# Two moves in a two-layer kernel: the position strips load behind the third time tile's twelfth slot tile, and the delta pairs are copied after the score masks

## The chip, the cores and the metric

The program runs on one core of one Trainium2 chip. The metric is device time of one execution in microseconds (us), the median of several runs. Before the change it is 2380.52 us (three runs, 2380.49 to 2381.03).

The core has five engines with their own instruction queues: TensorE (PE in the profile; its weight loads are PEld), VectorE (DVE), ScalarE (ACT), GpSimd (POOL) and SyncE (SP). Each works through its queue in the order in which the program was written out; an instruction that waits holds up everything behind it on its engine. DMA transfers are issued from SP's and from POOL's queue. The profile counts them as two DMA queues, q1 (hardware, SP) and q0 (software, POOL), served by 16 DMA engines.

## The reference

The input is `x`, 8 batches of 512 positions by 256 features, float32. Two transformer-like layers follow each other:

- Layer 0, attention: a delta-rule recurrence over the 512 positions with a 16 by 16 state for each of 16 heads and 8 batches (`delta = v - M k`, `M += beta k delta`, output `q M`), then RMS norm and a projection.
- Layer 0, feed-forward: a top-1 router over 8 experts, each 256 to 1024 to 256 with relu.
- Layer 1, attention: causal softmax attention with a relative position bias looked up by distance.
- Layer 1, feed-forward: 8 experts of 256 by 256, weighted by a thresholded softmax.

Before each part there is a layer norm with shift and scale from a small modulation matrix, and behind each a gated residual sum.

## The kernel before

**Time tiles.** The 512 positions are cut into four time tiles of 128 (`i` = 0 to 3; "the third time tile" is i = 2). `scan(i)` runs the recurrence of one tile, 128 steps of four VectorE operations each, for all batches and heads at once. While VectorE scans tile i, the other engines do the rest for tile i-1, cut into pieces with a due time in scan steps. `run` sorts the pieces by due time and issues a piece behind the scan step that it is due at. The scan of tile 3 is the last one; what is left of tile 2, all of tile 3's attention and routing, and then tile 3's experts come behind it, in the order of their due times alone.

**What follows a tile's scan** (`follow`): `attend(i)` turns keys and queries (`turn`, L593 writes `qT`), makes scores (`scores`, L607), masks them and copies the delta pairs (`mask`), weighs them (`weigh`, L663), projects, and adds to the residual rows `x1` (`rest`, L722 and L723); POOL then stores each batch's rows `x1[b]` to HBM (L724). The rows were loaded from the input by `tokens` (L563, on SP). For tiles 0 to 2, ScalarE copies the scores out of PSUM and POOL masks them (L642) and copies the pairs (L630). For tile 3, VectorE does both (L644 and L630). There is one `pair` tile, which `weigh` of the batch before still reads.

`route(i)` normalises `x1` in place (L781 on ScalarE, which must wait until the store L724 of that batch has read the rows), makes the router's logits, ranks the rows by expert and scatters them by an indirect DMA (L895) into 15 *slot tiles* of 128 rows, each of one expert.

`experts(i)` goes over the 15 slot tiles `j`: load the rows (L928, on SP, two buffers), turn them (L931), first expert matrix (L943), relu (L952), second matrix (L961), bias (L967, POOL), store (L968, POOL). The expert's two weight matrices, 1.05 and 1.18 MB, are fetched for each slot tile by indirect DMAs from POOL (L916), two buffers each. In the scan of tile 3 the slot tiles 0 to 11 of tile 2 are due from step 73 on, 4.3 steps apart; slot tiles 12, 13 and 14 (`rest`) are due at 58, 68 and 71 behind the scan.

**Gathers.** A tile's expert outputs are gathered back row by row (L976), multiplied by the gate (L1005) and added into the residual rows in HBM by an accumulating DMA (L1006), all issued by POOL, with two buffers `yrow`. For tiles 0 and 1 this is 16 gathers, and all of them stand behind the last scan, right behind slot tile 11 of tile 2 in POOL's order.

**Layer 1's constants.** `load1` (due at step 54 of the last scan) loads layer 1's weights. The position bias comes as `strips`, one row of 16 heads by 512 distances for each partition, 4.19 MB in all. `load_strips(p0)` loads it for 8 partitions at a time (L1070 on SP: 256 KB as 128 pieces of 2 KB), 16 loads. They are due at steps 56, 60, ... 116 of the last scan. The strips are read first by layer 1's scores (L1148). `place1` later loads layer 1's expert weights `ew` (L278, two loads of 1 MB on SP). The first rows for layer 1, `xs_first`, are loaded on SP (L972), and their statistics are made by VectorE (L186).

Of the kernel before, what the change touches and what calls it, by code (L numbers as in the profile page):

```python
# [19 lines left out]
P = 128  # L20
B = 8
S = 512
D = 256
NH = 16
# [6 lines left out]
STRIP = 640  # L31
# [26 lines left out]
COPIES = 8  # L58
# [5 lines left out]
def tile_two_layers(ctx: ExitStack, tc: tile.TileContext, t: dict, out: bass.AP):  # L64
    nc = tc.nc
# [9 lines left out]
    def bank():  # L75
        n_ps[0] += 1
        return banks[0].tile([P, 512], F32, tag="ps", name=f"ps{n_ps[0]}")
# [5 lines left out]
    strip_d = dram.tile([NH, COPIES, STRIP], F32, tag="strip_d", name="strip_d")  # L83
    hs_d = [dram.tile([NSLOT * P, D], F32, tag=f"hs{i}", name=f"hs{i}") for i in range(NT)]
# [17 lines left out]
    with tc.tile_pool(name="setup", bufs=2) as sp:  # L102
        for layer in range(2):
# [9 lines left out]
            for branch in range(2):  # L113
                for part in range(2):
# [11 lines left out]
                    got = pm[:, : 2 * B].rearrange("p (h b) -> p h b", h=2)  # L126
# [92 lines left out]
    w1 = {}  # L219
# [131 lines left out]
    with ExitStack() as l0:  # L351
# [11 lines left out]
        def free(i):  # L363

            return nc.vector if i == NT - 1 else nc.gpsimd
# [34 lines left out]
        pair = w0.tile([P, NH // 2, 3, HD], F32, name="pair")  # L400
# [152 lines left out]
        def attend(i, qk, V, x1, norms):  # L553
# [3 lines left out]
            got = {}  # L557
            ve = free(i)
# [68 lines left out]

            def mask(b):
                psts = got["s", b]
                ve.tensor_copy(  # L630
                    pair[:, :, 0:3:2, :],
                    got["dtok"][:, b * NH : (b + 1) * NH, :].rearrange(
                        "p (j o) d -> p j o d", o=2
                    ),
                )
                sts = []
                for r in range(4):
                    st = ap.tile([P, 4, P], F32, tag="stk", name=f"stk{i}_{b}_{r}", bufs=4)
                    before = strict.unsqueeze(1).to_broadcast([P, 4, P])
                    if i < NT - 1:  # L640
                        nc.scalar.copy(st, psts[r].rearrange("p (h t) -> p h t", h=4))  # L641
                        nc.gpsimd.tensor_mul(st, st, before)  # L642
                    else:
                        nc.vector.tensor_mul(  # L644
                            st, psts[r].rearrange("p (h t) -> p h t", h=4), before
                        )
                    sts.append(st)
                got["st", b] = sts

            def weigh(b):  # L650
# [85 lines left out]
            pieces = [(0, deltas), (1, tokens)]  # L736
# [18 lines left out]
        issued = {}  # L755
# [147 lines left out]
        def experts(i, slot, idx):  # L903
# [7 lines left out]
            def fetch(j, part):  # L911
                if j >= NSLOT:
                    return
                first, n = (0, WONE) if part == 0 else (WONE, WROW - WONE)
                w = fp.tile([P, n], F32, tag=f"w{part}", name=f"w{part}_{i}_{j}", bufs=2)
                issued["fetch"] = nc.gpsimd.indirect_dma_start(  # L916
                    out=w,
                    out_offset=None,
                    in_=t[f"wrows{part}"],
                    in_offset=bass.IndirectOffsetOnAxis(ap=idx[:, j : j + 1], axis=0),  # L920
                ).ins
                ws[j, part] = w
# [2 lines left out]
                fetch(j, part)  # L925
            for j in range(NSLOT):
                hr = fp.tile([P, D], F32, tag="hslot", name=f"hslot{i}_{j}", bufs=2)
                nc.sync.dma_start(hr, hs_d[i][j * P : (j + 1) * P, :])  # L928
                pt = bank()
                for c in range(2):  # L930
                    nc.tensor.transpose(  # L931
                        pt[:, c * P : (c + 1) * P], hr[:, c * P : (c + 1) * P], ident
                    )
                hT = fp.tile([P, 2, P], F32, tag="hTs", name=f"hTs{i}_{j}", bufs=2)
                nc.scalar.copy(hT, pt[:, :D].rearrange("p (c t) -> p c t", c=2))  # L935
                act = fp.tile([P, NFC, P], F32, tag="act", name=f"act{i}_{j}")
                w = ws[j, 0]
                for half in range(2):
                    ph = bank()
                    for q in range(4):  # L940
                        f = half * 4 + q
                        for k in range(2):
                            nc.tensor.matmul(  # L943
                                ph[:, q * P : (q + 1) * P],
                                w[:, k * FF + f * P : k * FF + (f + 1) * P],
                                hT[:, k, :],
                                start=(k == 0),
                                stop=(k == 1),
                            )
                    for q in range(4):  # L950
                        f = half * 4 + q
                        nc.scalar.activation(  # L952
                            act[:, f, :], ph[:, q * P : (q + 1) * P], AF.Relu,
                            bias=w[:, 2 * FF + f : 2 * FF + f + 1],
                        )
                fetch(j + 1, 1)
                yield
                w = ws[j, 1]
                py = bank()
                for f in range(NFC):  # L960
                    nc.tensor.matmul(  # L961
                        py[:, :D], act[:, f, :], w[:, f * D : (f + 1) * D],
                        start=(f == 0), stop=(f == NFC - 1),
                    )
                ysb = fp.tile([P, D], F32, tag="ysb", name=f"ysb{i}_{j}", bufs=2)
                nc.scalar.copy(ysb, py[:, :D])
                nc.gpsimd.tensor_add(ysb, ysb, w[:, NFC * D :])  # L967
                nc.gpsimd.dma_start(ys_d[i][j * P : (j + 1) * P, :], ysb)  # L968
                fetch(j + 2, 0)
                if i == NT - 1 and j == NSLOT // 2:  # L970
                    for k in range(i):
                        nc.sync.dma_start(w1["xs"][:, k, :], x2d[0][k])  # L972
                yield
# [9 lines left out]
            if i == NT - 1:  # L983
                rows = [w1["rows"][:, b * D : (b + 1) * D] for b in range(B)]
# [24 lines left out]
        def follow(i, qk, V):  # L1009
# [13 lines left out]
            def settle():  # L1023
                work["experts"] = experts(i, *next(work["route"]))
# [42 lines left out]
            w1["xs"] = wp1.tile([P, NT, D], F32, name="xs_first")  # L1067

        def load_strips(p0):
            nc.sync.dma_start(  # L1070
                w1["strips"][p0 : p0 + COPIES],
                bass.AP(
                    strip_d.tensor,
                    strip_d.offset + P - 1 - p0,
                    [[STRIP - 1, COPIES], [COPIES * STRIP, NH], [1, S]],
                ),
            )

# [3 lines left out]
        def run(pieces, steps=None):  # L1082
            left = sorted(pieces, key=lambda piece: piece[0])
            for s, step in enumerate(steps or ()):
                while left and left[0][0] <= s:
                    with tc.issue_after(step):
                        left.pop(0)[1]()
            for _, piece in left:
                piece()

        parts, pieces = front(0, 0)
        run(pieces)
        rest, gathers = [], []
        for i in range(NT):
            pieces = rest
            if i > 0:
                last = i == NT - 1
                more, rest, behind = follow(i - 1, before["qk"], before["V"])
                gathers += behind
                pieces = pieces + more  # L1100
                if last:
                    pieces = pieces + [(54, load1)] + [
                        (56 + p0 // 2, lambda p0=p0: load_strips(p0)) for p0 in range(0, P, COPIES)
                    ]
            before = parts
            if i + 1 < NT:
                parts, more = front(i + 1, 47 if i > 0 else 2)
                pieces = pieces + more
            run(pieces, scan(i, before["K"], before["V"]))
        more, last, _ = follow(NT - 1, before["qk"], before["V"])  # L1110
        run(rest + gathers + more)
        place1()
        first = {}
        begun = list(prologue(0, first, w1["xs"], (tuple(range(NT - 1)), (NT - 1,))))
# [9 lines left out]
    with ExitStack() as l1:  # L1124
        lp = l1.enter_context(tc.tile_pool(name="layer1", bufs=2))

        strips, wp, bp = (w1[key] for key in ("strips", "wp", "bp"))
# [68 lines left out]
        def tail(b, got):  # L1196
# [122 lines left out]
            for i in range(NT):  # L1319
                yield lambda i=i: experts(i)  # L1320

        got = [first] + [{} for _ in range(1, B)]
# [5 lines left out]
        for n in range(B * STEP + NT + 1):  # L1328
            b, m = divmod(n, STEP)
            if m == NT + 2:  # L1330
                if b + 1 < B:
# [127 lines left out]
```

## Time and profile before

| what | value |
|---|---|
| median of the runs | 2380.52 us |
| the profiled execution's own time | 2393.79 us |
| its span from first to last instruction | 2392.0 us |
| mean granted TensorE clock | 0.868 |
| PE busy | 1782.5 us (75%) |
| DVE busy | 1599.4 us (67%) |
| ACT busy | 1075.5 us (45%) |
| POOL busy | 646.3 us (27%) |
| last scan step (L540, last of 512) | starts at 1161.2 us |
| first score of layer 1 (L1148) | 1487.3 us |
| the 16 strip loads (L1070) issued | 994.3 to 1149.2 us |

A page counts the busy time of each engine over the whole span, and the busy share of an engine is a mean over stages with different limits. The stages here are: setup and the first tile's projections, four scans (to 1161 us), tile 3's attention, routing and experts behind them (to about 1487 us), and layer 1 (to the end). Times below are microseconds from the start of the span. "Idle before <- releaser" gives how long an engine stood idle before an instruction and whose end released it; a suffix q is the engine's queue, which issues DMAs and waits.

### The profile page before, as it was taken

The numbers are of one execution on the slowest core, as the hardware profiler recorded it, in microseconds if no ns is written. First come the engines' busy times: TensorE is split into PE (matmuls) and PEld (weight loads), VectorE is DVE, ScalarE is ACT, GpSimd is POOL, SyncE is SP. The second block draws the span as 40 slices with busy tenths as digits, with TensorE's granted clock in tenths as the row PEclk, the third lists the DMA queues.
The fourth block names the chain that finished last, engine by engine and source line by source line (L and its number), as shares of the span: only waits on it lengthen the run. The fifth ranks groups of instructions, "written<-read, shape, count | busy, mean of one in ns | idle before, by whom it ended". The sixth has DMA issues, their size and how long they took to land. (4 is left out here: it accounts for less than half of the span.)

```text
span 2392.0 us, 32119 instructions
## 1 busy us (share of the span) xinstructions
PE 1782.5 (75%) x10874; PEld 1221.9 (51%) x10874; DVE 1599.4 (67%) x4608; ACT 1075.5 (45%) x2579; POOL 646.3 (27%) x804
## 2 busy tenths in 40 slices
PE   6450006569677787857867787999998899999996
PEld 3220005348565675756746676554545454545553
DVE  2499999989997799799443002676666666666653
ACT  3561004554356443522322234874737374646531
POOL 0211006234462544633462643000100001010111
PEclk9675557689888997879987998999999999999997
DMA  5010000067312681449943884000000000000000
GB/s 184 17 47 0 0 0 9 15 221 265 137 54 96 232 290 52 107 148 261 310 76 107 265 317 130 17 3 14 10 9 15 21 4 21 3 21 5 10 10 9
DMA packets 82676, 209.91 MB, mean 88 GB/s; under 512 B 10248, under 2 KB 58544, under 8 KB 66896
## 3 DMA queue, kind: packets, MB, share of 16 engines
q0 software_dynamic: 29232, 158.47, 20.0%
q1 hardware_dynamic: 53280, 49.40, 7.1%
q8 instruction: 86, 1.41, 0.2%
q14 instruction: 78, 0.64, 0.1%
HBM read 175.10 MB, written 32.74 MB: 87 GB/s over the span
## 5 line engine op out<-in xcount | busy, mean ns | idle before, releaser
L1153 ACT ACTIVATE pr<-sc,low 128x384 f32<-128x384 f32 (+3 forms) x512 | 255.8, 556 | 266.7 <-DVE low L1148 264.6
L943 PE MATMUL ps<-hTs,w 128*128 128x128 f32 x1920 | 245.9, 290 | 51.0 <-ACT hTs L935 28.4
L1148 DVE CUSTOM_DVE_ANT_0 sc<-ps,strips 128x384 f32<-128x384 f32 (+3 forms) x512 | 226.6, 485 | 64.8 <-PE ps L1139 52.0
L943 PEld LDWEIGHTS ps<-hTs,w 128*128 128x128 f32 x1920 | 234.8, 203 | 65.1 <-ACT hTs L935 42.5
L540 DVE TENSOR_REDUCE state<-terms 128x16 f32<-128x272 f32 x512 | 227.3, 444 | 15.7
L961 PE MATMUL ps<-w,act 128*128 128x256 f32 x960 | 221.9, 385 | 18.0 <-ACT act L952 8.8
L551 DVE TENSOR_TENSOR state<-state,upd 128x256 f32<-128x256 f32 x511 | 220.5, 432 | 17.2
L1301 PE MATMUL ps<-ew,hTd 128*128 128x512 f32 x512 | 230.9, 604 | 0.0
L952 ACT ACTIVATE act<-ps,w 128x128 f32<-128x128 f32 x480 | 136.8, 368 | 194.4 <-PE ps L943 112.9
L546 DVE TENSOR_TENSOR upd<-K,state 128x256 f32<-128x256 f32 x511 | 214.0, 419 | 14.9
L536 DVE TENSOR_TENSOR terms<-state,K 128x256 f32<-128x256 f32 x512 | 214.7, 419 | 12.0
L1165 PE MATMUL ps<-cst,pr 128*128 128x128 f32 x1280 | 193.2, 296 | 13.7 <-DVE low L1148 11.6
L961 PEld LDWEIGHTS ps<-w,act 128*128 128x128 f32 x960 | 180.5, 192 | 44.4 <-ACT act L952 12.6
L1306 DVE SCALAR_TENSOR_TENSOR accd<-ps,wtd,accd 128x256 f32<-128x256 f32 x256 | 123.7, 483 | 118.9 <-PE ps L1301 74.6
L1165 PEld LDWEIGHTS ps<-cst,pr 128*128 128x128 f32 x1280 | 149.7, 149 | 87.3 <-issue 35.5
L1310 POOL TENSOR_TENSOR accd<-accd,bc_g 128x256 f32<-128x256 f32 x32 | 23.3, 727 | 562.7 <-DVE accd L1306 562.7
L916 POOL DMA_INDIRECT w<-in_wrows,idx x120 | 117.4, 978 | 168.3 <-ACT act L952 136.7
L1301 PEld LDWEIGHTS ps<-ew,hTd 128*128 128x128 f32 x512 | 95.6, 192 | 119.8 <-issue 106.1
L570 PE MATMUL ps<-cst,V 128*128 128x128 f32 x64 | 13.0, 385 | 169.4 <-DVE V L542 169.4
L1139 PE MATMUL ps<-kT,qTc 32*128 32x128 f32 (+3 forms) x1024 | 131.4, 500 | 9.8 <-DVE v L317 6.8
L642 POOL TENSOR_TENSOR stk<-stk,cst 128x512 f32<-128x512 f32 x96 | 119.2, 1267 | 19.0 <-ACT stk L641 16.8
L1174 DVE COPY prT<-ps 128x512 f32<-128x512 f32 (+3 forms) x256 | 117.6, 483 | 5.3 <-PE ps L1165 5.1
(238 smaller groups left out, 3038.8 us busy)
## 6 DMA issues: line engine op xcount, KB each, us to landing
hs<-zero SPq DMA_DIRECT2D x4, 1920.0 KB
hslot<-hs SPq DMA_DIRECT2D x60, 128.0 KB
ys<-ysb POOLq DMA_DIRECT2D x60, 128.0 KB
xt<-in_x SPq DMA_DIRECT2D x16, 256.0 KB
x<-in_x SPq DMA_DIRECT2D x32, 128.0 KB
x<-x POOLq DMA_DIRECT2D x32, 128.0 KB
strips<-strip_d SPq DMA_DIRECT2D x16, 256.0 KB
out<-accd SPq DMA_DIRECT2D x32, 128.0 KB
```

What stands on the lines that cost most here:

```text
L536: nc.vector.tensor_mul(term[:, :, :HD], M, K[:, s, :].unsqueeze(1).to_broadcast([P, HD, HD]))
L540: nc.vector.tensor_reduce(delta, term, AX.X, ALU.add)
L546: nc.vector.tensor_mul(upd, K[:, s, :].unsqueeze(2).to_broadcast([P, HD, HD]), delta.unsqueeze(1).to_broadcast([P, HD, HD]),)
L551: yield nc.vector.tensor_sub(M, M, upd).ins
L943: nc.tensor.matmul(ph[:, q * P : (q + 1) * P], w[:, k * FF + f * P : k * FF + (f + 1) * P], hT[:, k, :], start=(k == 0), stop=(k == 1),)
L952: nc.scalar.activation(act[:, f, :], ph[:, q * P : (q + 1) * P], AF.Relu, bias=w[:, 2 * FF + f : 2 * FF + f + 1],)
L961: nc.tensor.matmul(py[:, :D], act[:, f, :], w[:, f * D : (f + 1) * D], start=(f == 0), stop=(f == NFC - 1),)
L1139: made = nc.tensor.matmul(pscs[r][:, :W], qT[rows, g, o, i * P : (i + 1) * P], kT[rows, g, :W], start=True, stop=True,)
L1148: nc.vector.tensor_tensor_reduce(out=sc[:, :W], in0=pscs[r][:, :W], in1=strips[:, n, S - W :], scale=1.0, scalar=3.0e38, op0=ALU.add, op1= ...
L1153: nc.scalar.activation(pr, sc[:, :W], AF.Exp, bias=low, scale=-1.0)
L1165: nc.tensor.transpose(pt[:, (i - j) * P : (i - j + 1) * P], prs[r, i][:, j * P : (j + 1) * P], ident,)
L1301: nc.tensor.matmul(pe, hT[:, k, cols], ew[:, k, e : e + 2, :], start=(k == 0), stop=(k == 1),)
```

## The change

Two edits. First, the 16 strip loads leave the last scan's list of pieces. They join the list that runs behind it, at due times 1 + p0/3 for first partition p0 (1, 3.7, ... 41), and each is tied to the last slot-row load issued by then (`issued["rows"]`), which is that of slot tile 11 of tile 2. Second, in `mask` the copy of the delta pairs is written behind the four masks and not ahead of them.

```diff
             def mask(b):
                 psts = got["s", b]
-                ve.tensor_copy(
-                    pair[:, :, 0:3:2, :],
-                    got["dtok"][:, b * NH : (b + 1) * NH, :].rearrange(
-                        "p (j o) d -> p j o d", o=2
-                    ),
-                )
                 sts = []
                 for r in range(4):
...
                     sts.append(st)
+                ve.tensor_copy(
+                    pair[:, :, 0:3:2, :],
+                    got["dtok"][:, b * NH : (b + 1) * NH, :].rearrange(
+                        "p (j o) d -> p j o d", o=2
+                    ),
+                )
                 got["st", b] = sts
...
                 hr = fp.tile([P, D], F32, tag="hslot", name=f"hslot{i}_{j}", bufs=2)
-                nc.sync.dma_start(hr, hs_d[i][j * P : (j + 1) * P, :])
+                issued["rows"] = nc.sync.dma_start(hr, hs_d[i][j * P : (j + 1) * P, :]).ins
...
         def load_strips(p0):
-            nc.sync.dma_start(
-                w1["strips"][p0 : p0 + COPIES],
+            with tc.issue_after(issued["rows"]):
+                nc.sync.dma_start(
+                    w1["strips"][p0 : p0 + COPIES],
...
                 if last:
-                    pieces = pieces + [(54, load1)] + [
-                        (56 + p0 // 2, lambda p0=p0: load_strips(p0)) for p0 in range(0, P, COPIES)
-                    ]
+                    pieces = pieces + [(54, load1)]
...
         more, last, _ = follow(NT - 1, before["qk"], before["V"])
-        run(rest + gathers + more)
+        strips = [
+            (1 + p0 / 3, lambda p0=p0: load_strips(p0)) for p0 in range(0, P, COPIES)
+        ]
+        run(rest + gathers + strips + more)
         place1()
```

The order in which the written-out program has its instructions, engine by engine, differs from the one before as follows (a scheduling pass decides it, not the source lines alone):

- SP: the eight `tokens` loads of tile 3 stand ahead of tile 2's slot rows (seven ahead of slot tile 0, the eighth behind slot tile 1) where they stood behind slot tile 11. The 16 strip loads stand in one row behind the load for slot tile 11. The two `ew` loads and the loads of `xs_first` for tiles 0 and 1 change places: `xs_first` now stands behind both `ew` loads and behind tile 2's last slot rows.
- POOL: the stores L724 of tile 3's batches 0 to 3 stand behind all 16 gathers; before, the first two stood behind the 14th gather and the next two behind the 15th. In batch 2 of tile 1 and batch 2 of tile 2 the pair copy stands behind the four masks. In slot tile 0 of tile 2 one weight fetch and one bias addition change places.
- VectorE: the pair copies and masks of tile 3 stand in the same order as before, copy first. The statistics of `xs_first` stand behind the router's pick of tile 3 and ahead of its count (L844).
- TensorE: two matmuls that rank tile 2's rows (L847, L851) stand behind the turn of one slot tile, and the same kind of exchange of two router matmuls of tile 3 with slot tile 12's turn. ScalarE: no difference.

More of the change, by code (lines that the diff above doesn't have):

```diff
@@ L1069, in load_strips @@
         def load_strips(p0):
-            nc.sync.dma_start(
-                w1["strips"][p0 : p0 + COPIES],
[L1072 to L1077, printed above, removed]
+            with tc.issue_after(issued["rows"]):
+                nc.sync.dma_start(
+                    w1["strips"][p0 : p0 + COPIES],
+                    bass.AP(
+                        strip_d.tensor,
+                        strip_d.offset + P - 1 - p0,
+                        [[STRIP - 1, COPIES], [COPIES * STRIP, NH], [1, S]],
+                    ),
+                )
         def run(pieces, steps=None):
```

## The prediction

> **What bounds the kernel now.** The last scan ends at 1162 us and layer 1 starts at 1487 us. The change touches only what lies between, and the slot tiles just before. I read the busy time by stretches first, with the DMA share.
>
> ```profile
> core 0: us, PE busy (x) PEld busy (x) DVE busy (x) ACT busy (x) POOL busy (x), PEclk, DMA share, GB/s
> 995.00:1010.00 15.00, 15.00 (x105) 12.90 (x104) 10.35 (x27) 7.01 (x22) 4.55 (x4) 0.67 0.54 82
> 1062.00:1120.00 58.00, 44.60 (x250) 40.11 (x250) 53.83 (x130) 14.27 (x49) 14.95 (x19) 0.85 0.94 261
> 1120.00:1162.00 42.00, 33.15 (x220) 29.74 (x220) 38.96 (x93) 12.36 (x43) 14.83 (x19) 1.00 0.99 298
> 1162.00:1184.00 22.00, 20.64 (x135) 18.66 (x135) 0.01 (x1) 8.28 (x29) 7.86 (x10) 1.00 1.00 358
> 1184.00:1232.00 48.00, 43.18 (x486) 32.55 (x484) 26.20 (x54) 19.49 (x54) 31.08 (x35) 0.93 0.49 117
> 1232.00:1251.00 19.00, 0.11 (x4) 0.00 (x0) 0.58 (x1) 3.15 (x9) 14.89 (x20) 0.63 0.44 90
> ```
>
> From 1062 to 1184 us, tile 2's slot tiles 0 to 11, the DMA engines are full (last two columns). Strips are a poor load: in 995 to 1010, where they are nearly alone, they move 82 GB/s and still take 0.54 of the engines. Then comes a stretch, 1232 to 1251, in which TensorE does nothing. TensorE's waits in the slot stage (us in total, times, longest), and one slot-row load on SP with the turn that waited for it:
>
> ```profile
> PE ps L943 <- DMA w<-in_wrows,idx: 8.6, 4, 4.3
> PE ps L931 <- DMA hslot<-hs: 6.6, 2, 5.4
> PE ps L961 <- DMA w<-in_wrows,idx: 3.5, 5, 1.7
> ```
>
> ```profile
> 1061.51 0.34 SPq L928 DMA_DIRECT2D hslot<-hs  x1
> ...
> 1085.66 0.44 PE L931 MATMUL ps<-cst,hslot 128*128 128x128 f32 x2 [1.27 <-DMA hslot<-hs]
> ```
>
> 128 KB took 24 us, behind two strips on the same queue. So the slot tiles run late: slot 11 ends at 1183.6, and only then TensorE starts tile 3's attention, whose input was ready at 1162. Then the idle 19 us, followed back through the timelines of TensorE, ScalarE and POOL:
>
> ```profile
> 1183.57 1.96 PE L570 MATMUL ps<-cst,V 128*128 128x128 f32 x16
> ...
> 1251.46 2.09 PE L607 MATMUL ps<-qT,kTa 32*128 32x256 f32 x16 [19.36 <-ACT qT L593]
> ```
>
> ```profile
> 1246.43 1.10 ACT L781 ACTIVATE x<-x,offf,rsf 128x256 f32<-128x256 f32 x2 [19.10 <-DMA x<-x]
> ```
>
> ```profile
> 1184.27 0.73 POOL L967 TENSOR_TENSOR ysb<-ysb,w 128x256 f32<-128x256 f32 x1 [1.61 <-ACT ysb L966]
> 1185.15 0.97 POOL L976 DMA_INDIRECT yrow<-ys,slot  x1 [0.15 <-issue]
> ...
> 1195.40 1.07 POOL L976 DMA_INDIRECT yrow<-ys,slot  x1 [2.51 <-DMA x<-yrow]
> ...
> 1236.80 1.05 POOL L976 DMA_INDIRECT yrow<-ys,slot  x1 [0.50 <-DMA x<-yrow]
> ...
> 1243.46 0.89 POOL L724 DMA_DIRECT2D x<-x  x1
> ```
>
> TensorE waits for ScalarE's `qT`, which is queued behind L781, which waits for the store L724, which POOL issues only after 14 gathers. That is the path: slot 11, gathers in pairs, L724, L781, TensorE. Attention itself was done at 1232 and is not on it.
>
> **The change part by part.** The sum is made in the profiled execution's time (2393.8 us, 13.3 over the median of 2380.5); I add the difference to the median unscaled.
>
> *Strips out of the slot stage.* 11 of the 16 leave the stretch from 1059 to 1184. TensorE's first matrix L943 starts at 1065.77 for slot 0 and at 1176.44 for slot 11: 110.7 us for 11 steps. The undisturbed rows are 1159.81, 1168.36, 1176.44, a mean of 8.3; the first step stays at 10.2 (slow clock). 10.2 + 10 x 8.3 = 93.2, so **-17.5**. Weights alone need 2.23 MB in 8.3 us, 269 GB/s, under the 358 of the last window, so TensorE sets this pace. Bounds: 0 (DMA stays the limit) to -17.5; I take the whole, since the windows show room.
>
> *TensorE's new order in tile 2's routing.* L847 now stands behind a turn (0.69) and its copy by ScalarE (wait 0.46): **+1.1**, on the path to the scatters and slot 0.
>
> *Strips behind slot 11's rows.* That load leaves SP when slot 9 has been turned, at about 1143. All 16 strips follow. At 82 GB/s 4.19 MB take at least 51 us, and until about 1195 they share with weights. For slots 10 and 11 the price lies between 0 and 2 x 7.1 = 14 (the worst step, 1086.56 to 1101.99, against 8.3); near the stage's mean of 10.06 it is 3.5, and part of slot 10's weights is already there: **+2**. L570 then starts at 1183.6 - 17.5 + 1.1 + 2 = 1169.2.
>
> *POOL's order.* From L570 to L724 is 59.9 us before, with 14 gathers. Now 16 stand ahead. A pair takes 8.0 (1195.40 to 1243.46 is six): **+8.0**. This is the step that turns the gain round.
>
> *Gathers under the strips.* They began at 1185 with strips gone; now at 1170 with strips until about 1230, some six of eight pairs. Per pair: 0 at least, no reason for a gain; at most 4.0, by tile 2's pairs beside full DMA engines (L976 at 1330.36, 1340.79, 1351.47, 1363.45: up to 12.0). I take 2, nearer the middle since those pairs also hold slot work on POOL: +12, and +2 for the first pair, which queues behind weights that are later than before: **+14** (0 to 32). L724 at 1169.2 + 59.9 + 8.0 + 14 = 1251.1 against 1243.46: **+7.6**.
>
> *The four stores together.* Before, a gather stood between them and L781 waited a second time (1.42). **-1.0** (0 to -1.4).
>
> *SP's order behind that.* The eight `tokens` loads now wait only for the scatters (L895, 1047 to 1057), as slot 0's rows must anyway: 0; if a scatter holds them, up to 8 x 0.34 = 2.7. Slot 12's rows queue behind the strips but are used at 1287: 0. `xs_first` leaves SP only after slot 12's turn (1287.3) and both `ew` loads. Its statistics, now ahead of L844 on VectorE, are hidden by L844's wait for L839 until 1297.5 (7.24 us idle). 1.4 MB at about 250 GB/s plus landing gives 1296: just covered, **+0.5** (0 to 3).
>
> *The second edit.* VectorE's order does not change, so tile 3 gets nothing. On POOL two pair copies (0.40 each) of tiles 1 and 2 go behind four masks (1.27 each); the scan on VectorE hides them. Without that cover: up to 5 us each. The exchange of a weight fetch and L967 in slot 0 delays that fetch by 3.6 us with 11 us to spare: 0. TensorE's exchange at slot 12: 0, up to 0.6.
>
> Sum: 7.6 - 1.0 + 0.5 = **+7.1 us**, 2387.6.
>
> [...] The row first: on SP's queue, two strips and a slot load, 0.66 MB, took 24 us beside weights while the whole stage moved 261 GB/s, so the weights kept most of the engines. [...]
>
> **The rivals.**
> - *Faster, the strips cost the gathers nothing.* The place is the gather chain, the price the 14 us. For it: the gathers' stage has a DMA share of only 0.49 and the pairs wait on latency. L724 at 1169.2 - 2 + 67.9 = 1235.1, so -8.4 - 1.0 = -9.4: 2371. It decides once the strips' two prices, 2 and 14, come to under 4 together. Against it: the first pair, beside weights, took 10.2 and not 8.0.
> - *Much slower, strips choke the weights.* Slots 10 and 11 lose 14, each pair 3 to 4: L724 at 1183.6 - 17.5 + 1.1 + 14 + 67.9 + 26 = 1275, +31: 2411. For it: the step from 1086.56 to 1101.99. Against: most strips in the stage cost about 1.7 us of a slot's step.
> - *Nothing in the end.* The gain of 15 to 17 at L570 and the losses behind it meet: within 5 us, 2380. This needs the two prices to come to between 4 and 13 together, not 16.
> - *The second edit does not do what it says* on VectorE: taken as certain from the order.
>
> **How the numbers follow.** Forecast with its neighbours (over +4.8) 0.45, much slower 0.13, nothing 0.21, faster 0.21. 0.2%, 4.8 us, is about what the measurement can tell from no change. Slower 0.58, same 0.21, faster 0.21. Range: down to the rival of no cost, 2371; up to +24, 2405, since both high bounds at once are unlikely. If slower, 2385 to 2405.
>
> **What would show it.** Right: the slot steps near 8.3, L570 near 1169, L724 of batch 0 near 1251 behind 16 gathers, TensorE idle some 40 us ahead of L607 with L593 and L781 as releasers, pairs near 10 us. Wrong: pairs at 8 us while strips run (faster), or waits of L943 and L961 for weights in slots 10 and 11 of several us (much slower). If VectorE waits for `xs_first` ahead of L844, the half microsecond was too little.

## The result, and the profile after

The changed kernel takes 2408.48 us (2404.34 to 2415.61, four runs) beside 2380.51 us for the kernel before: a ratio of 1.0123, 95% interval 1.0097 to 1.0149. A second comparison gave 1.0076 (1.0059 to 1.0092), and the same kernel without its second edit 1.0082 (1.0057 to 1.0107). The forecast, 2387.6 us, is a ratio of 1.0030: the direction is right, but the loss is two and a half to four times as large (18 to 28 us for 7). The kernel before itself took 2379 to 2389 us from one comparison to the next, so only ratios are compared from here on.

The profiled execution took 2415.61 us, with a span of 2413.8 us. One profile's positions are good to some 10 us: in a second profile of the changed kernel layer 1's first score comes at 1494.3 us and not 1504.7. Lengths inside a stage agree far better (L570 to L724 takes 89.6 and 88.6 us in the two), and the readings below rest on them.

The stretches that the prediction showed, now of the kernel after (us, busy times of the five engines, clock, DMA share, GB/s):

```profile
core 0: us, PE busy (x) PEld busy (x) DVE busy (x) ACT busy (x) POOL busy (x), PEclk, DMA share, GB/s
995.00:1010.00 15.00, 15.00 (x103) 12.39 (x104) 8.88 (x24) 6.96 (x22) 4.03 (x5) 0.76 0.08 18
1062.00:1120.00 58.00, 54.33 (x348) 49.75 (x349) 53.84 (x130) 20.14 (x69) 20.42 (x25) 0.96 0.85 311
1120.00:1162.00 42.00, 32.84 (x205) 29.05 (x204) 35.82 (x86) 12.42 (x42) 13.36 (x17) 0.92 0.93 267
1162.00:1184.00 22.00, 18.54 (x170) 15.22 (x174) 5.55 (x10) 10.10 (x26) 7.88 (x11) 1.00 0.85 233
1184.00:1232.00 48.00, 29.79 (x373) 22.61 (x368) 19.07 (x45) 11.99 (x38) 20.02 (x23) 0.85 0.55 105
1232.00:1251.00 19.00, 0.00 (x0) 0.00 (x0) 0.00 (x0) 0.00 (x0) 14.36 (x17) 0.50 0.41 68
```

From 1062 to 1120 us TensorE is busy 54.3 us instead of 44.6, and the engines move 311 GB/s instead of 261: without strips, TensorE sets the pace. From 1120 us, with strips, less is moved (267 for 298, 233 for 358 GB/s). The empty stretch of TensorE is longer. The slot stage's end, in TensorE's timeline (start, duration, instruction, wait):

```profile
1137.31 3.84 PE L943 MATMUL ps<-hTs,w 128*128 128x128 f32 x32 [0.59 <-ACT hTs L935]
...
1145.51 3.81 PE L943 MATMUL ps<-hTs,w 128*128 128x128 f32 x32 [0.69 <-DMA w<-in_wrows,idx]
1155.51 5.57 PE L961 MATMUL ps<-w,act 128*128 128x256 f32 x16 [6.19 <-DMA w<-in_wrows,idx]
...
1161.87 3.84 PE L943 MATMUL ps<-hTs,w 128*128 128x128 f32 x32 [0.56 <-ACT hTs L935]
...
1169.47 1.96 PE L570 MATMUL ps<-cst,V 128*128 128x128 f32 x16
...
1265.56 2.09 PE L607 MATMUL ps<-qT,kTa 32*128 32x256 f32 x16 [51.39 <-ACT qT L593]
```

Slot tiles 1 to 9 take 8.1 us each; slot tile 10, the first beside strips, takes 16.4 us. L570 starts 14.1 us earlier than before. Then TensorE is idle for 51.4 us ahead of L607, where it was 19.4. As before, `qT` stands behind L781 on ScalarE, and L781 waits for the stores L724:

```profile
1262.12 2.07 ACT L781 ACTIVATE x<-x,offf,rsf 128x256 f32<-128x256 f32 x4 [52.64 <-DMA x<-x]
```

POOL's timeline has the reason (the first gather of pairs one to four, the first product of pairs one and two, and what each waited for):

```profile
1171.06 0.97 POOL L976 DMA_INDIRECT yrow<-ys,slot  x1 [0.15 <-issue]
...
1182.49 0.72 POOL L1005 TENSOR_TENSOR yrow<-yrow,gate 128x256 f32<-128x256 f32 x1 [7.34 <-DMA yrow<-ys,slot]
...
1196.09 1.07 POOL L976 DMA_INDIRECT yrow<-ys,slot  x1 [9.57 <-DMA x<-yrow]
...
1208.12 0.73 POOL L1005 TENSOR_TENSOR yrow<-yrow,gate 128x256 f32<-128x256 f32 x1 [9.51 <-DMA yrow<-ys,slot]
...
1215.15 1.05 POOL L976 DMA_INDIRECT yrow<-ys,slot  x1 [3.04 <-DMA x<-yrow]
...
1222.37 1.06 POOL L976 DMA_INDIRECT yrow<-ys,slot  x1 [0.35 <-DMA x<-yrow]
...
1259.08 2.52 POOL L724 DMA_DIRECT2D x<-x  x4
```

The first pair takes 25.0 us, the second 19.1, the next five 7.2 to 7.7 each. POOL does little else meanwhile (a store L968 and a weight fetch L916 behind the first gathers): it waits for the gathered rows and for the accumulating DMAs to land. The trace's DMA records, one for each piece that was moved, show the last strip piece at 1213.1 us, 2 us before the second pair ends. The first store L724 is 15.6 us later than before.

From here the 15.6 us are only carried on: layer 1's first score moves by 17.4 us. Over eleven profiles, here and below, of kernels that load the strips before L724 and leave the gathers in one chain, it follows the first store by 237 to 246 us, and layer 1 takes 901 to 910 us from it to the end. The changed kernel's 245.7 and 909.1 lie at the upper end of both ranges; those of before are 243.9 and 904.7. From the first store to layer 1's first score, the four profiles with the strips moved (this one, its repetition, `strips_only` and `aligned`) have a mean of 241.5 us, and the two with the strips in their old place (before and `mask_only`) 241.5 us too. So nothing of the loss is found between L724 and layer 1. What the times show beyond 13 to 16 us is within the scatter of single executions (2374 to 2396 us for the kernel before in one comparison), and no step is known for it.

### The profile page after: what moved, and what is told of

Read it like the earlier page. It is cut to its first block, busy times and chain, and to the rows that moved or that the text cites. A ratio compares the mean times of both kernels' runs of the same rounds, so it can differ in the third digit from the quotient of the medians.

```text
span 2413.8 us, 32119 instructions
## 1 busy us (share of the span) xinstructions
PE 1783.6 (74%) x10874; PEld 1220.2 (51%) x10874; DVE 1598.9 (66%) x4608; ACT 1076.2 (45%) x2579; POOL 646.5 (27%) x804
## 5 line engine op out<-in xcount | busy, mean ns | idle before, releaser
L961 PE MATMUL ps<-w,act 128*128 128x256 f32 x960 | 224.5, 388 | 17.2 <-DMA w<-in_wrows,idx 15.4
L551 DVE TENSOR_TENSOR state<-state,upd 128x256 f32<-128x256 f32 x511 | 220.7, 432 | 17.2
L961 PEld LDWEIGHTS ps<-w,act 128*128 128x128 f32 x960 | 182.7, 195 | 43.5 <-issue 16.8
L916 POOL DMA_INDIRECT w<-in_wrows,idx x120 | 117.4, 979 | 142.5 <-ACT act L952 110.7
L570 PE MATMUL ps<-cst,V 128*128 128x128 f32 x64 | 12.9, 385 | 169.4 <-DVE V L542 169.4
L636 POOL TENSOR_TENSOR stk<-stk,cst 128x512 f32<-128x512 f32 x96 | 119.3, 1270 | 18.4 <-ACT stk L635 16.1
```

What stands on the lines that cost most here:

```text
L551: yield nc.vector.tensor_sub(M, M, upd).ins
L961: nc.tensor.matmul(py[:, :D], act[:, f, :], w[:, f * D : (f + 1) * D], start=(f == 0), stop=(f == NFC - 1),)
```

## The experiments

Two lengths measure what the strips cost: the step of slot tile 10 (8.1 us undisturbed) and the time from L570 to L724. Ratios are to the kernel before, with a 95% interval. Each run has a label, by which it is named later.

**Each edit alone.** First the strips alone (`strips_only`: the mask edit undone):

> The strips alone are moved; the delta pairs are copied ahead of the masks as before. Theory (all of the loss comes from the strips and from the order of POOL's queue that follows from them): as the changed kernel, 2408 us, and the first store L724 of tile 3 at 1259 us in the trace. Rival (part of the loss comes from the masks ahead of the copies on POOL, in tiles 1 and 2): at least 5 us less, under 2403 us.

1.0082 (1.0057 to 1.0107); slot tile 10's step 15.8 us, first pairs 24.7 and 21.8 us, L724 at 1257.7 us. Then the second edit alone, in the kernel before (`mask_only`):

> The kernel before with the second edit alone. Theory (VectorE's order does not change, on POOL two batches change under the scan): 2380.5 us within 5 us. Rival (the second edit costs or gains something by itself): more than 5 us from 2380.5 us, and L570 of tile 3 shifted by that amount against 1183.6 us.

1.0002 (0.9974 to 1.0030), L724 at 1243.7 us. The strips are the whole of the loss; the second edit does nothing that can be measured.

**The change once more, and aligned rows.** First the changed kernel again (`after_again`):

> The changed kernel itself, once more beside the kernel before on the chip of the next three. Theory (the loss stands at layer 1's first score, 17 us later, and layer 1 takes the same time as before): 1.007 to 1.010 of the kernel before, some 17 to 24 us, and layer 1 from its first score to the end within 5 us of the 906.6 us of before. Rival (layer 1 itself takes 5 to 10 us longer): 1.011 or more, and layer 1 longer by over 5 us in this profile too.

1.0076. Slot tile 10's step is 16.1 us, the first pairs 25.0 and 18.2 us, L570 to L724 88.6 us (89.6 in the first profile). Layer 1 takes 901.3 us against 904.7, from the first score itself (the expectation counts from a wait 1.9 us ahead of it). The rival is out: layer 1 is not longer.

Then every strip row read from an aligned place (`aligned`):

```diff
-                        strip_d.offset + P - 1 - p0,
-                        [[STRIP - 1, COPIES], [COPIES * STRIP, NH], [1, S]],
+                        strip_d.offset,
+                        [[STRIP, COPIES], [COPIES * STRIP, NH], [1, S]],
```

> The changed kernel, but every strip row is read at the same distance from a 2560-byte boundary (partition stride 640 elements and not 639), so that the position bias is not the reference's; as many bytes and pieces of 2 KB as before, in the same place. Theory (a strip load is slow because only 8 partitions, and so half of the engines, serve it): as the changed kernel, strips until about 1213 us, first two pairs of gathers 40 to 46 us, L724 at 1255 to 1261 us, 2400 to 2410 us. Rival (a strip piece is slow because each row starts 4 bytes further on than the last): pieces well under 212 ns, the strips end by 1195 us, L724 at 1245 us or earlier, the time 10 us or more under the changed kernel.

1.0069 (1.0028 to 1.0110), last strip piece at 1210.7 us, first pairs 25.6 and 17.2 us. Where the rows start makes no difference that can be measured.

**The gathers without strips.** The strips leave only behind tile 2's last slot tile (`strips_late`):

```diff
-            (1 + p0 / 3, lambda p0=p0: load_strips(p0)) for p0 in range(0, P, COPIES)
+            (72 + p0 / 100, lambda p0=p0: load_strips(p0)) for p0 in range(0, P, COPIES)
```

> The changed kernel with the 16 strip loads due behind tile 2's last slot tile, so that they leave SP only at about 1280 us: neither slot tiles 0 to 11 nor the gathers meet them. 16 gathers still stand ahead of the stores. Theory (the strips beside the weights and the gathers make the first two pairs of gathers long): L570 at about 1167 us, the pairs 10 us, then 7.5 to 8 us each, L724 at 1233 to 1236 us, some 24 us ahead of the changed kernel; the total then near 2371 us plus what the strips cost tile 3's slot tiles, 2370 to 2385 us. Rival (the first pairs are long because they start earlier, behind the weights of slot tiles 12 and 13 on their own queue, strips or not): pairs of about 25 and 19 us also here, L724 at 1256 us or later, the total 2400 us or more.

POOL's timeline of this kernel, the first gather of pairs one to three, and the stores:

```profile
1157.28 0.97 POOL L976 DMA_INDIRECT yrow<-ys,slot  x1 [0.15 <-issue]
...
1167.57 1.08 POOL L976 DMA_INDIRECT yrow<-ys,slot  x1 [2.86 <-DMA x<-yrow]
...
1174.98 1.05 POOL L976 DMA_INDIRECT yrow<-ys,slot  x1 [0.48 <-DMA x<-yrow]
...
1221.94 2.53 POOL L724 DMA_DIRECT2D x<-x  x4
```

The first two pairs take 10.3 and 7.4 us here, with the weights of slot tiles 12 and 13 ahead of them on their queue as always. The rival is out: an early start alone does not make them long. Slot tile 10's step is 8.1 us, and L570 to L724 takes 66.2 us with 16 gathers. So POOL's new order costs 6.3 us (66.2 against 59.9), and the strips cost the gathers 23.4 us (89.6 against 66.2).

The total is not the theory's, and is over the rival's 2400 us for another reason: 1.0172 (1.0118 to 1.0225). What is gained until L724 is lost where the strips now run, as the waits from 1255 to 1380 us show (total, times, longest):

```profile
DVE stc L186 <- DMA xs_first<-x: 90.8, 1, 90.8
ACT hTs L935 <- PE ps L931: 69.2, 3, 67.1
PEld ps L931 <- DMA hslot<-hs: 67.3, 1, 67.3
```

Tile 3's slot rows and `x_last` stand behind the strips on SP and leave only at 1367 us; tile 3's first slot tile starts at 1371 us.

**The weights ahead of the first pair.** The weights of slot tiles 12 and 13 are fetched only behind the first four stores (`fetch_held`):

```diff
+                if i == NT - 2 and j == 12:
+                    with tc.issue_after(issued["store"]):
+                        for held in ((12, 0), (12, 1), (13, 0)):
+                            fetch(*held)
...
-                fetch(j + 1, 1)
+                if i != NT - 2 or j != 11:
+                    fetch(j + 1, 1)
...
-                fetch(j + 2, 0)
+                if i != NT - 2 or j not in (10, 11):
+                    fetch(j + 2, 0)
...
-                    with tc.issue_after(issued["scatter" if i == NT - 2 else "fetch"]):
+                    with tc.issue_after(issued["scatter" if i == NT - 2 else "ys"]):
```

(`issued["ys"]` is the last store L968, here that of slot tile 11.)

> The changed kernel with the weights of slot tiles 12 and 13 of tile 2 fetched only behind the first four stores L724, so that the first pair of gathers has strips beside it and no weights on its own queue. Theory (part of the first pair's 25 us is the weights ahead of it on its queue, made late by the strips): first pair 15 to 19 us, second pair 8 to 19 us, L724 at 1243 to 1252 us. Rival 1 (the strips slow the gathers' own pieces, weights or not): first pair 23 to 26 us, L724 at 1256 us or later. Rival 2 (only the queue counts): first pair 10 to 11 us, second 7.5 us, L724 at 1236 to 1239 us. The time moves with L724 at most, since the late weights may hold slot tile 12.

POOL's timeline (L984 is the gather here, L1013 the gate's product):

```profile
1164.47 1.02 POOL L984 DMA_INDIRECT yrow<-ys,slot  x1 [0.30 <-issue]
...
1174.41 0.73 POOL L1013 TENSOR_TENSOR yrow<-yrow,gate 128x256 f32<-128x256 f32 x1 [7.64 <-DMA yrow<-ys,slot]
...
1186.29 1.07 POOL L984 DMA_INDIRECT yrow<-ys,slot  x1 [7.86 <-DMA x<-yrow]
...
1200.11 1.05 POOL L984 DMA_INDIRECT yrow<-ys,slot  x1 [0.50 <-DMA x<-yrow]
```

The first pair takes 21.8 us, between theory and first rival, and the second 13.8 us (the strips end at 1195.0 us); L570 to L724 takes 83.6 us. Weights without strips made it 10.3, strips without those weights 21.8, both together 25.0. So most of the price is the strips against the gathers' own pieces; weights made late on the gathers' queue add some 3 us. The time, 1.0070 (1.0042 to 1.0099), hardly moves.

**POOL's order.** The last pair of gathers tied behind the first four stores (`stores_first`; `issued["store"]` is the last L724 written by then):

```diff
+                    key = "scatter" if i == NT - 2 else "fetch"
+                    if i == 1 and b >= 6:
+                        key = "store"
-                    with tc.issue_after(issued["scatter" if i == NT - 2 else "fetch"]):
+                    with tc.issue_after(issued[key]):
```

> The changed kernel, with the last pair of gathers tied behind the first four stores L724 of tile 3, so that 14 gathers stand ahead of the stores and not 16. Theory (the chain of gathers on POOL is the path): the stores come one pair earlier, L724 at 1251.5 us and not 1259.1 us, and the time falls by 7 to 8 us to about 2401 us. Rival (the path at that place is another, or the gain is given back behind it): L724 earlier, but the time within 3 us of the changed kernel's 2408 us.

L724 comes at 1254.5 us behind 14 gathers, later than the theory's 1251.5: the second pair takes 23.5 us here, and L570 to L724 86.5 us for 88.6 and 89.6. The ratio is 1.0052 (1.0025 to 1.0079), 7 us under the 1.0082 of `strips_only` in the same comparison, but the intervals overlap, so this run alone does not settle it. Then all eight gathers of tile 1 (`gathers_split`):

```diff
+                    key = {0: "fetch", 1: "store", 2: "scatter"}[i]
...
-            at, apart = [(1, 2.2), (21, 2.2), (100, 2), (0, 0)][i]
+            at, apart = [(1, 2.2), (31.5, 1.5), (100, 2), (0, 0)][i]
```

> The changed kernel with the eight gathers of tile 1 tied behind the first four stores L724 of tile 3: 8 gathers ahead of the stores and not 16. Theory (POOL's chain of gathers alone holds the stores): L724 at 1230 to 1234 us, some 27 us ahead of the changed kernel, and TensorE's idle time ahead of L607 shorter by as much; the time 20 to 28 us under the changed kernel, 2380 to 2388 us. Rival (the second half of tile 3's attention, whose stores now stand behind the other eight gathers, gives it back): the last four stores no earlier than 1280 us, the time within 8 us of the changed kernel.

L724 at 1227.5 us, TensorE's idle time ahead of L607 22.3 us for 51.4, ratio 0.9977 (0.9958 to 0.9996): 24 us under the changed kernel. The chain of gathers is the path, and pairs five to eight need not stand on it. The same split in the kernel before, with the strips in their old place (`before_split`):

> The kernel before, with the eight gathers of tile 1 tied behind the first four stores L724 of tile 3; strips as before, among tile 2's slot rows. Theory (the chain of gathers on POOL is the path to L724): L724 at 1218 to 1224 us and not 1243.5 us, the time 18 to 24 us under before (ratio 0.990 to 0.9925). Rival (the other eight gathers then hold the last four stores, and it is given back): the time within 5 us of before.

L724 at 1217.8 us, TensorE's long wait at L607 is gone, and the ratio is 0.9945 (0.9912 to 0.9978), 13 us (5 to 21) where 18 to 24 were expected. A possible reason, not tested, is that the last four stores now wait behind tile 1's gathers until 1254.4 us, 8 us after VectorE's last L723.

**Other places.** In the kernel before, the strips in one row behind tile 1's last slot-row load (`early8b`; tied to `issued["rows"]` as in the change):

```diff
-                        (56 + p0 // 2, lambda p0=p0: load_strips(p0)) for p0 in range(0, P, COPIES)
+                        (66.2 + p0 / 1000, lambda p0=p0: load_strips(p0)) for p0 in range(0, P, COPIES)
```

> The kernel before with the 16 strip loads in one row behind the slot-row load of tile 1's last slot tile, at about 1003 us, ahead of tile 2's slot tiles. Copy order of the masks as before, 14 gathers ahead of the first stores. Theory (strips are cheap where the DMA engines have room, dear beside weights and gathers): strips end near 1055 us, slot steps 8.1 us each, L570 at 1157 to 1162 us, pairs of gathers 10 and then 7.8 us, L724 at 1215 to 1220 us, 23 to 28 us ahead of before, and the time 2355 to 2362 us on a chip where the kernel before takes 2380.5 us (ratio 0.989 to 0.993). Rival (the strips delay tile 2's attention, scatters or first weights by as much as they free): slot tile 0 later than 1075 us and the time within 5 us of before.

0.9960 (0.9938 to 0.9981). The slot steps are 8.07 us and the first pairs 9.9 and 8.4, as in theory, but the scan ends 6 us later than before, L570 comes at 1170.0 and L724 at 1227.3 us, and the gain is about half of the theory's: tile 2's routing is late, and VectorE waits for its logits.

```profile
DVE lg L819 <- PE ps L804: 9.8, 1, 9.8
```

Next, meant for the gap of the DMA engines before tile 2's slot tiles (in the kernel before, a share of 0.00 at 1 GB/s from 1030 to 1047 us), with `COPIES = 16`, alone (`hole16`) and with the split (`hole16_split`); a column that ScalarE copies into `strips` holds the loads back:

```diff
+        def mark():
+            with tc.issue_after(issued["relu"]):
+                nc.scalar.copy(w1["strips"][:, 0, 0:1], issued["act"][:, NFC - 1, 0:1])
...
-                    pieces = pieces + [(54, load1)] + [
+                    pieces = pieces + [(54, load1), (66.4, mark)] + [
```

> The kernel before with eight strip loads of 16 partitions, which wait on ScalarE's relu of tile 1's slot tile 14 (through one copied column) and so leave SP at about 1027 us, when the DMA engines have nothing to do until 1047 us. 14 gathers ahead of the stores as before. Theory (strips cost nothing where no weights and gathers run): strips end by about 1060 us, slot tile 0's L943 at 1062 to 1070 us, slot steps 8.1 us, L570 at 1161 to 1169 us, L724 at 1219 to 1229 us, ratio 0.990 to 0.994. Rival (they delay the scatters and first weights by as much as they free): slot tile 0 at 1080 us or later, ratio over 0.997.

> Both together: strips of 16 partitions in the gap at about 1027 us, and the eight gathers of tile 1 behind the first four stores of tile 3. Theory (the two gains add, since both shorten the same path): L724 at 1200 to 1207 us, ratio 0.981 to 0.986. Rival (the attention itself or the last four stores are the path then): L724 held by VectorE's L723, or the last four stores late, ratio 0.988 or more.

1.0056 (1.0030 to 1.0081) and 0.9987 (0.9961 to 1.0012): the ratios are the rivals'. That relu came at 1042 us and not at 1027, when the gap was nearly over; the strips ran from 1044 to 1091 us, and slot tile 0 started at 1094 us. Its rows stood behind 4.19 MB on SP's queue (`hole16`; 48.3 us in `hole16_split`, so there too it was the strips, and not the stores):

```profile
PE ps L931 <- DMA hslot<-hs: 48.0, 1, 48.0
```

**What makes a strip dear.** Strips on 16 partitions for each load, at the changed kernel's place (`copies16`: `COPIES = 16` for 8):

> The changed kernel with 16 partitions for each strip load and not 8, so 8 loads of 512 KB, in the same place. Theory (a load of 8 partitions keeps only half of the DMA engines busy, and 16 partitions spread over all): the strips end before 1195 us and not at 1213 us, the second pair of gathers takes 8 to 10 us and not 19, L724 at 1245 to 1250 us, the time 8 to 14 us under the changed kernel. Rival (the price is the bytes and descriptors, whatever the engines): strips until about 1213 us, first two pairs 44 us together, the time within 4 us of the changed kernel.

1.0040 (1.0017 to 1.0063). The strips end at 1201.4 us, not before 1195, so the second pair is undisturbed (7.3 us); but slot tile 10's step is 18.8 us and the first pair 26.8. L570 to L724 takes 80.8 us, where 66.2 were taken without strips: a shorter, denser load moves more of the price than it removes. Then only the partitions that a load writes, with 8 partitions (`spread8`) and with 16 (`spread16`):

```diff
-                    w1["strips"][p0 : p0 + COPIES],
+                    w1["strips"][p0 // COPIES : P : P // COPIES],
...
-                        strip_d.offset + P - 1 - p0,
-                        [[STRIP - 1, COPIES], [COPIES * STRIP, NH], [1, S]],
+                        strip_d.offset + P - 1 - p0 // COPIES,
+                        [[STRIP - P // COPIES, COPIES], [COPIES * STRIP, NH], [1, S]],
```

> The changed kernel with the same 16 strip loads of 8 partitions in the same place, but each load writes partitions 16 apart (0, 16, 32, ...) and not 8 neighbours; what is computed is the same. Theory (a strip piece of 2 KB takes 212 to 250 ns because eight neighbouring partitions are written at once): strip pieces near 100 ns, strips done by 1185 us, first two pairs of gathers under 30 us together, L724 at 1246 us or earlier, the time 10 us or more under the changed kernel. Rival (the price is on the reading side or in the piece itself): strips until about 1210 us, first two pairs 40 to 46 us, the time within 4 us of the changed kernel.

> The changed kernel with 8 strip loads of 16 partitions, each 8 apart (0, 8, 16, ...), in the same place. Theory (neighbouring partitions are what makes the piece slow): DMA share in 1140 to 1200 us below 1, strips done by 1175 us, slot tile 10's step under 12 us, first pair under 18 us, L724 at 1240 us or earlier. Rival (reading side or piece): as with 16 neighbouring partitions, first pair 25 to 28 us and L724 at 1250 to 1256 us.

With 8 partitions, 16 apart: 1.0014 (0.9988 to 1.0039), slot tile 10's step 13.2 us, pairs 20.0 and 19.8, strips until 1204 us: the strips and the pairs are nearer to the rival. With 16 partitions, 8 apart: 0.9989 (0.9960 to 1.0018), step 12.4 us, pairs 18.6 and 8.3, strips until 1169.9 us, L724 at 1224.9 us, L570 to L724 73.1 us: but for a step and a first pair just over its bounds, the theory. The slot stage's end and the stretch behind it, first for 16 neighbouring partitions:

```profile
core 0: us, PE busy (x) PEld busy (x) DVE busy (x) ACT busy (x) POOL busy (x), PEclk, DMA share, GB/s
1137.00:1162.00 25.00, 16.06 (x93) 14.35 (x94) 20.30 (x49) 5.67 (x20) 6.50 (x8) 0.81 1.03 233
1162.00:1184.00 22.00, 18.41 (x128) 14.97 (x131) 2.78 (x5) 8.98 (x21) 7.49 (x9) 0.82 1.02 257
```

and for 16 partitions 8 apart:

```profile
1137.00:1162.00 25.00, 20.30 (x129) 16.99 (x130) 12.12 (x27) 8.96 (x21) 8.12 (x10) 0.86 1.03 326
1162.00:1184.00 22.00, 21.66 (x275) 16.81 (x273) 11.10 (x21) 9.24 (x30) 11.13 (x13) 1.00 0.57 137
```

As many engines are busy (1.03), but they move 326 GB/s instead of 233. In the DMA records a strip piece of 2 KB takes a mean of 119 ns for 182, and a weight piece (8 to 9 KB), from the first strip to the last, 436 ns for 551. So it is the neighbouring partitions that make strips slow, and that slow what runs beside them. For `spread8` the chain explains about 6 of the 15 us gained against the second comparison (whose interval is some 7 us wide each way); the rest is not shown.

**Both terms away.** Early strips and split gathers (`early8b_split`):

> The strips in one row behind the slot-row load of tile 1's last slot tile (about 1000 us), and the eight gathers of tile 1 behind the first four stores of tile 3. Theory (the strips' bill on the slot stage and the gathers' order are two separate terms of one path, so they add): L570 at 1170 us, L724 at 1203 to 1208 us, layer 1's first score at 1446 to 1452 us, ratio to the kernel before 0.985 to 0.989. Rival (the other eight gathers hold the last four stores and take one gain back): the last store L724 at 1250 us or later, ratio 0.992 or more.

0.9926 (0.9893 to 0.9958), L570 at 1163.4 us, L724 at 1199.5 us, the last stores at 1236.6 us: a smaller gain than the theory's, though the stores are not late as the rival had it. The product of the two single ratios, 0.9960 x 0.9945 = 0.9905, lies in the interval: the terms add, within what was measured.

The same with strip loads of 16 partitions (`early16b_split`):

> As the run before it, with strip loads of 16 partitions: 8 loads that use all DMA engines for some 30 us instead of half of them for some 55 us. Theory (a strip piece takes about 250 ns wherever it is, so the bill is the same in sum, and only who pays it moves: slot tile 14 of tile 1 waits longer, slot tile 0 of tile 2 less): last scan step and slot tile 0 within 4 us of the run before, ratio within 0.3% of it. Rival (ending sooner frees the first weights): slot tile 0's L943 5 us earlier or more, ratio 0.3% lower.

0.9887 (0.9828 to 0.9945): slot tile 0 is 5.8 us earlier (1058.9 us), as the rival had it, but the intervals overlap.

And with these 16 partitions 8 apart (`early16b_split_spread`):

> Strip loads of 16 partitions, 8 apart, behind the slot-row load of tile 1's last slot tile, and the eight gathers of tile 1 behind the first four stores of tile 3. Theory (neighbouring partitions are what makes the piece slow): the strips end before 1015 us, VectorE does not wait at L819 (12.5 us with neighbours), the scan's last step at 1150 us or earlier, ratio to the kernel before 0.980 to 0.985. Rival (reading side or piece): as with neighbours, last scan step at 1156 us, ratio 0.986 to 0.992.

0.9848 (0.9811 to 0.9885), 2349.54 us where the kernel before took 2389.03: the lowest ratio of all. From 998 to 1003 us practically nothing but strips is moved in this run and in `early16b_split`: a piece takes 178 ns for 302, and the core moves 195 GB/s for 117, so neighbouring partitions are slow by themselves too. The strips end at 1021.5 us for 1029.5, VectorE waits 2.9 us at L819 and not 12.5, and L607 follows in TensorE's timeline without the long gap:

```profile
1154.22 2.07 PE L570 MATMUL ps<-cst,V 128*128 128x128 f32 x16
...
1189.78 1.15 PE L607 MATMUL ps<-qT,kTa 32*128 32x256 f32 x16
1196.32 1.15 PE L607 MATMUL ps<-qT,kTa 32*128 32x256 f32 x16
```

The theory wanted the strips done before 1015 us and the last scan step by 1150 us; that step is at 1153.4, halfway to the rival's 1156. The ratio is the theory's, but its interval overlaps that of `early16b_split`, so what the spread is worth at this place is not shown by the time.

## Why the prediction was right or wrong

- **Strips out of the slot stage, -17.5, and TensorE's order, +1.1.** Measured together -22.9 (the undisturbed step is 8.07 us, not 8.3; from slot tile 0 to 10 it takes 83.2 us against 102.6; and slot tile 0 starts 3.5 us earlier instead of later, which is within the scatter of positions, so the +1.1 is neither shown nor ruled out). "TensorE sets this pace" holds.
- **Strips behind slot 11's rows, +2.** Wrong size: +8.8 (8.3 in slot tile 10, 0.5 in 11), inside the stated 0 to 14. The part of slot tile 10's weights that was not yet there held L961 for 6.2 us. It met the error above, so that L570 came at 1169.5 us where 1169.2 was forecast: two errors, not one good step.
- **POOL's order, +8.0.** Right in mechanism; 6.3 us.
- **Gathers under the strips, +14: the step that failed.** It measured 23.4 us (22.4 in the second profile). The upper bound for a pair, 4.0 us, came from pairs beside full DMA engines with weights only. The first pair lost 14.7 us and the second 11.7; the others lost nothing. (26.4 us, less 3 by which the later ones beat those of strips_late.) The price was spread over six pairs at a rate, but the strips were done by 1213 us, not 1230, and took it all from those that ran beside them. The measured terms are stretches of one path and add up to the first store's delay: -22.9 + 8.8 + 6.3 + 23.4 = +15.6, where +7.6 was forecast. What the first comparison's 28 us have beyond that is not explained by any step.
- **The four stores together, -1.0.** From L724 to L607 it takes 6.5 us and not 8.0: -1.5.
- **`xs_first`, +0.5.** Hidden, as forecast: VectorE's wait for it was over at 1310.8 us, and L844 could not start before 1312.6.
- **The second edit, 0.** Shown (1.0002).
- **The row on SP's queue.** The row, one slot-row load that took 24 us behind two strips, was read as weights keeping the engines. The runs show the opposite: how slow strips are, and what they do to weights. In the first profile of the changed kernel the whole core moves 143 GB/s from 1140 to 1146 us, when the strips have just begun, and weight pieces (8 to 9 KB) take a mean of 910 ns where they take 397 in the 18 us up to 1138; in the second profile it is 140 GB/s, 993 and 388 ns. So strip pieces on SP's queue lengthen the pieces on POOL's.

Of the rivals, "much slower" had the right mechanism and two prices near the measured ones (14 for slot tiles 10 and 11 and 26 for the gathers, against 8.8 and 23.4). The lower end of the range rested on strips that cost the gathers nothing; even in `spread16`, their cheapest form at this place, they cost 6.9 us (73.1 against 66.2).

## What to carry to other kernels

Before a slow transfer is moved, ask what will run beside it at the new place and how many dependent DMA round trips that has: here two pairs of gathers lost 26 us to 4.19 MB that cost the kernel far less 140 us earlier (`early8b`, 0.9960). A bound from a busy stretch is only good for the same kind of traffic (4.0 us a pair was taken here, and the first pair lost 14.7); 82 GB/s at 0.54 of the DMA share was the sign that these pieces are of another kind. And a chain on one queue (POOL's gathers ahead of the stores) is worth cutting before anything is moved around it (`before_split`, 0.9945).

## What the runs showed of the hardware

- Loads of eight partitions nearly alone fill 0.54 of the DMA engines at 82 GB/s (the kernel before, 995 to 1010 us); those of sixteen 1.07 at 144 GB/s (`hole16`, 1044 to 1056 us). The 2 KB piece takes a mean of 227 ns in the first case and 253 ns in the second; with sixteen and practically nothing else, 302 ns at 117 GB/s (`early16b_split`, 998 to 1003 us).
- With sixteen partitions 8 apart the piece takes 119 ns beside weights and gathers (`spread16`), with sixteen neighbours 182 ns (`copies16`); with practically nothing beside it 178 (`early16b_split_spread`) and 302 ns (`early16b_split`). Weight pieces beside the strips move with it: 436 ns in `spread16`, 551 ns in `copies16`.
- At the changed kernel's place the ratio falls from eight neighbouring partitions (1.0076, `after_again`) over sixteen neighbours (1.0040, `copies16`) and eight 16 apart (1.0014, `spread8`) to sixteen 8 apart (0.9989, `spread16`); each of the four intervals overlaps the next. Why neighbouring partitions are slow is not shown, and no other spacing was tried.
